# A recurrent block followed by cross attention: the attention's contexts dealt out over four steps instead of three

## The chip, the cores and the metric

The kernel runs on one core of one Trainium2 chip, in float32. The metric is the device time of one execution in microseconds; several executions are timed and the median is given. One further execution is taken by the hardware profiler.

The core's engines are called as in the profile: PE (TensorE, matrix multiplies and transposes), PEld (its weight loads), DVE (VectorE), ACT (ScalarE), POOL (GpSimd) and SP (SyncE, which issues all DMA transfers of this kernel, in order).

## The reference

The input `x` has 16 sequences of 128 tokens with 512 channels. Layer 0 is a recurrent block, layer 1 an attention between the channels of `x` and a second input `ctx` of the same shape (which also gives layer 0 its state). Cut to what matters:

```python
# layer 0
xa  = ln(x);  sx = shift(xa) - xa
xxx = einsum(tanh((xa + sx*maa_x) @ maa_w1), maa_w2)       # five mixtures
xk, xw, xv, xr, xg = xa + sx * (maa_stack + xxx)
w = exp(-exp(time_decay + tanh(xw @ td_w1) @ td_w2))
r, k, v, g = xr @ Wr.T, xk @ Wk.T, xv @ Wv.T, silu(xg @ Wg.T)
for t in range(128):                                       # 32 heads of 16
    out_t = r_t @ (u * k_t v_t + s);  s = k_t v_t + w_t * s
x1 = x + groupnorm(out) * g @ Wo.T
xc = ln(x1);  sx2 = shift(xc) - xc
x2 = x1 + sigmoid((xc + sx2*fr) @ Wfr.T) * (relu((xc + sx2*fk) @ Wfk.T)**2 @ Wfv.T)
# layer 1, per sequence; 128 "channels" x 512 "positions"
Mn = Wn @ inorm(x2) + bn
Mm = Wm @ inorm(ctx) + bm
A  = softmax(Mn.T @ Mm)
return Wo @ ((Wl @ ctx + bl) @ A.T) + bo + x2
```

What hangs on `ctx` alone in layer 1, `Mm` and the product of `Wo`, `Wl` and `ctx`, is called a context here. It does not depend on layer 0.

## The kernel before

The 16 sequences form 8 groups of two (`n = 2`, `G = 8`). A group passes through stages, each a generator that yields between portions:

- `stageB` (L227): first norm, shift and the matmuls `p1` (L245, L249) of the mixtures.
- `stageB2` (L268): the five mixtures `px` (L286), the projections `pj` (L224) with Wk, Wr, Wg and `pv` (L331) with Wv, and the decay (`pd`, `pw`).
- `stageR` (L358): the recurrence, in a form with pair products, masks and small matmuls (`pq` L405, `p4` L410, `pl` L456, `pu` L505, `pa` L526, `po` L533 and L538). It loads the state `s0` (L381), spreads keys into KX by eight DMAs (L425) and values into VX by four (L474).
- `stageC` (L568): transposes `py` (L580), the output projection and the channel mix: `ptk` (L594) with Wo, Wfr and Wfv, `pj` (L621) with Wfk.
- `stageX` (L759): loads a group's contexts back from DRAM.
- `stageL` and `stageLb` (L810, L772): the attention: `pn` (L779), and four times per sequence the scores `pS` (L785), their maximum on DVE (L787), the exponential on ACT (L789), the reciprocal (L790), scaling (L791), the transpose `pA` (L794) and its eviction (L797); after each second one `pO` (L803) and an addition (L805).
- `stageE` (L752) calls `context` (L732) for each sequence of the groups that it is given.

A context loads the sequence into `xs` (L737), takes statistics on DVE (L131, in `rownorm`, with a power on POOL) and normalizes on ACT (L145). `pm` (L741) and its eviction with bias (L742) give one half of `MVe`, four matmuls `pV` (L746) and a copy (L747) the other; L749 stores it to DRAM as `mvD`, of which there are 16. `xs` and `MVe` have no room of their own: by the number of the sequence in the group, they take the tiles of `yT` or `xk2`, and of `xcT` or `sx2`, which `stageC` uses otherwise. The two PSUM banks are those of the attention (`ls` and `la`):

```python
xs = sb1.tile([128, 512], FP, name="xs", tag=("yT", "xk2")[i])
mv = sb1.tile([128, 1024], FP, name="MVe", tag=("xcT", "sx2")[i])
```

The work goes in steps. Group g is in stage B at step g, in B2 at g + 1, R at g + 2, C at g + 3, X and L at g + 4; the last group's C and L are written apart (`stageCb`) and run at step 10, next to the second last group's attention. Within a step, `interleave` (L823) takes portions of the step's streams by a due time, which is the stream's delay (`DLY`) plus the share of its portions done. The contexts come with a delay of 1, after the others:

```python
if step in EARLY:
    gs = EARLY[step]
    streams.append((stageE(gs), 2 * len(gs), 1, (6, step)))
```

This is the order in which the instructions are traced. A scheduler then gives each engine its order: what was traced earlier comes first, but an instruction whose operands and buffers are free in the scheduler's own timing is drawn ahead. So work of a later portion can fill the gaps of an earlier one, across steps too. The engines then run these orders as they stand.

Of the kernel before, what the change touches and what calls it, by code (L numbers as in the profile page):

```python
# [26 lines left out]
OFF = [0, 1, 2, 3, 4, 4]  # L27
ORDER = [3, 4, 2, 1, 0, 5]
DLY = [-0.2, 0.2, 0.0, 0.4, 0.8, 0.4]
EARLY = {0: [0, 1], 1: [2, 3], 2: [4, 5, 6, 7]}  # L30
LASTX = 2


# [1 line left out]
def rwkv_xattn_kernel(ctx: ExitStack, tc: tile.TileContext, a: dict, out: bass.AP):  # L35
# [716 lines left out]
    def stageE(gs):  # L752

        for g in gs:
            for b in range(n):
                context(g, b)
                yield
# [87 lines left out]
    for step in range(G + max(OFF)):  # L845
# [5 lines left out]
        for k in ORDER:  # L851
            for g in range(G):
                if step_of(k, g) == step and not (g == G - 1 and k in (3, 4)):
                    streams.append((ST[k][0](g), ST[k][1], DLY[k], (k, g)))
# [3 lines that stand above are left out]
# [72 lines left out]
```

## Time and profile before

| | us |
|---|---|
| median of 3 runs | 971.24 |
| lowest and highest | 967.41, 981.34 |
| the profiled execution | 969.33 |
| its span (first to last instruction) | 967.5 |
| PE busy | 898.5 (93%) |
| DVE busy | 644.3 (67%) |
| ACT busy | 500.4 (52%) |
| first and last start of a context's `pm` | 21.2, 154.4 |
| first `pS` of the attention | 272.7 |

Busy times come from one profiled execution. The difference of span and time lies before the first and after the last instruction. A matmul in float32 is two entries on PE, and a run of them overlaps, so their lengths add up to more than the time that they take; the spacing of their starts is the time that counts.

In the views, `out<-in` names the tiles by the program's names without buffer numbers, and what stands behind an arrow in brackets is what ended an idle time.

### The profile page before, as it was taken

To read this page: it belongs to the slowest core of one execution; us is meant where nothing else is said; L and a number is where in the kernel's file an instruction comes from. 1 tells how busy PE (TensorE), PEld (TensorE's weight loads), DVE (VectorE), ACT (ScalarE), POOL (GpSimd) and SP (SyncE) were. 2 spreads that over 40 slices of the span, in tenths; PEclk is the share of its full clock that TensorE was granted. 3 is DMA by queue.
4 is the path that set the end of the run, shared out by engine and by line. 5 is a ranking of instruction groups with operands and counts; after the bars stand their busy time and mean duration, and the time that the engine had idled before them with its cause. 6 is when DMAs were issued, how large, how long until landed. Compare 5 with 4: busy or idle time off the path is not lost.

```text
span 967.5 us, 19263 instructions
## 1 busy us (share of the span) xinstructions
PE 898.5 (93%) x7556; PEld 613.0 (63%) x7556; DVE 644.3 (67%) x1599; ACT 500.4 (52%) x1057; POOL 59.2 (6%) x95
## 2 busy tenths in 40 slices
PE   4889999998989999999999999999989998997985
PEld 3666767667554867576756677585846565754643
DVE  5787677946586668875787578755784595942322
ACT  4675273443366445564565445734564265654544
POOL 5111010000000000010000000000000000000000
PEclk9999999999999999999999999999999999998998
DMA  6566647355413635253444524553445323344410
GB/s 200 182 239 215 200 154 247 96 158 190 142 55 72 206 123 179 60 173 110 140 115 132 190 86 131 147 182 102 131 112 145 139 66 113 96 155 142 152 44 23
DMA packets 77612, 134.04 MB, mean 139 GB/s; under 512 B 33825, under 2 KB 43681, under 8 KB 77520
## 3 DMA queue, kind: packets, MB, share of 16 engines
q1 hardware_dynamic: 77522, 132.81, 44.5%
q8 instruction: 60, 0.98, 0.4%
q14 instruction: 30, 0.25, 0.1%
HBM read 104.45 MB, written 22.04 MB: 131 GB/s over the span
## 4 chain that ended last, share of the span: by engine, by line
PE 64%; DVE 18%; ACT 7%; DMA 6%; SPq 3%; issue 2%; POOL 0%; DVEq 0%; ACTq 0%; POOLq 0%
PE ptk L594 14%; PE pj L224 11%; PE pv L331 5%; PE pj L621 5%; PE pO L803 4%; PE pl L456 4%; PE pS L785 4%; DVE PP L394 3%; PE pA L794 2%; PE ptl L674 2%; SPq L425 2%; DVE xm L289 2%; PE pu L505 1%; DVE xm L290 1%; PE po L533 1%
## 5 line engine op out<-in xcount | busy, mean ns | idle before, releaser
L224 PE MATMUL pj<-xm,wb 128*128 128x256 f32 x768 | 179.4, 386 | 2.9 <-DVE xm L289 2.8
L224 PEld LDWEIGHTS pj<-xm,wb 128*128 128x128 f32 x768 | 145.3, 193 | 28.3 <-issue 5.7
L143 POOL TENSOR_TENSOR rs<-rs,mhalf 128x1 f32<-128x1 f32 x64 | 40.8, 644 | 619.2 <-DVE rs L128 605.0
L785 PE MATMUL pS<-MV,Mn 128*128 128x512 f32 x112 | 62.9, 644 | 9.1 <-ACT e L789 5.2
L789 ACT ACTIVATE e<-pS,nm 128x512 f32<-128x512 f32 x64 | 44.3, 693 | 50.1 <-DVE nm L787 49.8
L787 DVE TENSOR_REDUCE nm<-pS 128x1 f32<-128x512 f32 x64 | 43.5, 685 | 40.1 <-PE pS L785 39.9
L803 PE MATMUL pO<-AT,MV 128*128 128x256 f32 x224 | 58.4, 399 | 1.9 <-ACT AT L797 1.9
L289 DVE TENSOR_TENSOR xm<-px,sx 128x512 f32<-128x512 f32 x80 | 53.6, 681 | 7.6 <-PE px L286 7.5
L331 PE MATMUL pv<-wb,xm 128*128 128x512 f32 x128 | 57.5, 597 | 0.2 <-DMA wb<-wvc 0.2
L797 ACT COPY AT<-pA 128x512 f32<-128x512 f32 x64 | 37.4, 585 | 39.1 <-PE pA L794 34.7
L791 ACT ACTIVATE e<-e,nm 128x512 f32<-128x512 f32 x64 | 46.4, 730 | 18.7 <-DVE nm L790 18.7
L290 DVE TENSOR_TENSOR xm<-xm,xaT 128x512 f32<-128x512 f32 x80 | 54.4, 684 | 0.5
L803 PEld LDWEIGHTS pO<-AT,MV 128*128 128x128 f32 x224 | 43.1, 198 | 17.8 <-issue 7.1
L621 PE MATMUL pj<-xk,wb 128*128 128x256 f32 x224 | 52.4, 383 | 0.0
L594 PE MATMUL ptk<-wb,kk 128*128 128x512 f32 x112 | 51.4, 596 | 0.9 <-DMA wb<-in_Wfv_dram 0.9
L456 PE MATMUL pl<-KX,r 128*32 128x128 f32 x1536 | 48.6, 274 | 3.3 <-DMA KX<-ks 3.0
L594 PE MATMUL ptk<-wb,sx 128*128 128x512 f32 x112 | 50.8, 598 | 0.0
L594 PE MATMUL ptk<-wb,yT 128*128 128x512 f32 x112 | 49.8, 596 | 0.8 <-DVE nm L790 0.8
L456 PEld LDWEIGHTS pl<-KX,r 128*32 128x32 f32 x1536 | 40.8, 110 | 14.1 <-issue 8.8
L794 PEld LDWEIGHTS pA<-ident,e 128*128 128x128 f32 x256 | 30.0, 141 | 30.6 <-issue 14.0
L805 DVE SCALAR_TENSOR_TENSOR x<-pO,cb,x 128x256 f32<-128x256 f32 x32 | 15.4, 480 | 49.5 <-PE pO L803 49.3
L286 PE MATMUL px<-sk,w2s 98*128 98x256 f32 x160 | 41.7, 356 | 5.4 <-ACT sk L264 2.0
(201 smaller groups left out, 1709.9 us busy)
## 6 DMA issues: line engine op xcount, KB each, us to landing
wb<-in_Wk_dram SPq DMA_DIRECT2D x16, 512.0 KB, 4.6
mvD<-MVe SPq DMA_DIRECT2D x16, 512.0 KB, 4.1
wb<-in_Wr_dram SPq DMA_DIRECT2D x16, 512.0 KB, 3.4
wb<-wvc SPq DMA_DIRECT2D x16, 512.0 KB, 3.6
wb<-in_Wg_dram SPq DMA_DIRECT2D x16, 512.0 KB, 4.2
wb<-in_Wo_dram SPq DMA_DIRECT2D x14, 512.0 KB, 3.4
wb<-in_Wfk_dram SPq DMA_DIRECT2D x14, 512.0 KB, 3.5
MV<-mvD SPq DMA_DIRECT2D x14, 512.0 KB, 3.8
```

The source lines that it names most:

```text
L224: nc.tensor.matmul(pj[:, m], lhsT=wb[:, m, cc, :], rhs=xm[:, cc], start=cc == 0, stop=cc == 3)
L289: nc.vector.tensor_tensor(xm[:, sl], px.rearrange("p c (b t) -> p c b t", b=n), sx[:, sl], ALU.mult)
L290: nc.vector.tensor_tensor(xm[:, sl], xm[:, sl], xaT[:, sl, :, 1:129], ALU.add)
L331: nc.tensor.matmul(pv, lhsT=xm[:, m, b], rhs=wbs[m // 2][:, m % 2], start=m == 0, stop=m == 3)
L456: nc.tensor.matmul(t[cs, 128 * cc : 128 * cc + 128], lhsT=r[:, cc, b, cs], rhs=KX[:, n * cc + b, :, 16 * c : 16 * c + 16], start=True, sto ...
L594: nc.tensor.matmul(pt, lhsT=act[:, m, b], rhs=wbs[m // 2][:, m % 2], start=m == 0, stop=m == 3)
L621: nc.tensor.matmul(pj[:, m], lhsT=wb[:, m, cc, :], rhs=xk2[:, cc], start=cc == 0, stop=cc == 3)
L785: nc.tensor.matmul(pS, lhsT=Mn[:, tsl], rhs=Mm, start=True, stop=True)
L789: nc.scalar.activation(e, pS, AF.Exp, bias=nm[:, 0:1], accum_out=nm[:, 1:2])
L791: nc.scalar.activation(e, e, AF.Identity, scale=nm[:, 2:3])
L794: nc.tensor.transpose(pA[:, sc], e[:, 128 * sc : 128 * sc + 128], ident)
L803: nc.tensor.matmul(pO, lhsT=Vc[:, sc], rhs=AT[:, sc], start=sc == 0, stop=sc == 3)
```

## The change

One table of the program is another one. Steps 0 to 2 had the contexts of two, two and four groups; now steps 0 to 3 have those of one, two, three and two groups. The code of a context, its tiles and its place in a step (after the others) are the same.

```diff
-EARLY = {0: [0, 1], 1: [2, 3], 2: [4, 5, 6, 7]}
+EARLY = {0: [0], 1: [1, 2], 2: [3, 4, 5], 3: [6, 7]}
```

Step 3 is the first in which `stageC` runs, for group 0.

## The prediction

> **What bounds the kernel now.** I read the profile's first page, then the busy times of each engine by stretches that follow the steps, then the instructions of the contexts, then TensorE's order of time where it stood still, and last the chain of waits. The page first: span, busy share of TensorE, and its busy tenths and granted clock over 40 slices of 24 us.
>
> ```profile
> span 967.5 us, 19263 instructions
> PE 898.5 (93%) x7556; PEld 613.0 (63%) x7556; DVE 644.3 (67%) x1599; ACT 500.4 (52%) x1057; POOL 59.2 (6%) x95
> PE   4889999998989999999999999999989998997985
> PEclk9999999999999999999999999999999999998998
> ```
>
> TensorE is busy 898.5 of 967.5 us; the other 69 us are at the start, in a few slices between, and at the end. The change moves matmuls and removes none, so the whole effect has to come out of these 69 us. The stretches say where they lie (length, busy time of TensorE, weight loads, VectorE, ScalarE, GpSimd, granted clock, DMA share):
>
> ```profile
> 0.00:100.00 100.00, 78.51 (x489) 56.03 (x490) 73.31 (x206) 57.81 (x115) 24.31 (x33) 0.97 0.65 212
> 100.00:160.00 60.00, 58.05 (x601) 44.23 (x600) 40.86 (x103) 29.73 (x63) 4.33 (x8) 0.99 0.60 189
> 160.00:230.00 70.00, 65.43 (x603) 48.06 (x603) 55.91 (x128) 26.41 (x65) 2.23 (x3) 0.96 0.56 162
> 260.00:300.00 40.00, 34.36 (x249) 20.22 (x247) 30.80 (x77) 25.32 (x58) 1.92 (x2) 0.96 0.21 54
> 300.00:500.00 200.00, 196.60 (x1794) 138.87 (x1794) 146.90 (x356) 105.47 (x227) 8.10 (x16) 1.00 0.45 138
> 800.00:968.00 168.00, 142.37 (x918) 87.68 (x916) 71.30 (x204) 87.59 (x180) 5.00 (x10) 0.95 0.32 104
> ```
>
> Length less busy gives TensorE's idle time: 21.5 us in the first 100, 2.0 in 100 to 160, 4.6 in 160 to 230, 5.6 in 260 to 300, 3.4 in 300 to 500 and 25.6 at the end; the stretches not shown hold the other 7. From 300 on TensorE sets the pace (98%), so work that comes late there costs its full length.
>
> Now the contexts: the two lines of their matmuls and statistics, with first and last start.
>
> ```profile
> L741 PE MATMUL pm<-l1n,wnm x32: 590/593/1223, 21.2 to 154.4; 128*128 128x512 f32 x32
> L131 DVE BATCH_NORM_STATS2 st<-xs x16: 656/690/695, 16.5 to 131.6; 128x6 f32<-128x512 f32 x16
> DMA to landing us min/median/max: 2.5/3.3/5.6
> ```
>
> All 16 contexts are through by 155 us (two `pm` passes each, so 32). They are filler: the first user, attention of group 0, starts near 271.
>
> TensorE around the gap before the second channel mix (start, length, instructions, and in brackets how long it stood idle before and for whom):
>
> ```profile
> 272.74 1.13 PE L785 MATMUL pS<-MV,Mn 128*128 128x512 f32 x2 [0.31 <-ACT Mn L781]
> 278.53 1.94 PE L785 MATMUL pS<-MV,Mn 128*128 128x512 f32 x2 [2.03 <-ACT e L789]
> 287.31 1.04 PE L580 MATMUL py<-ident,y 128*128 128x128 f32 x8
> 289.83 1.06 PE L405 MATMUL pq<-PP,emat 128*32 128x512 f32 x8 [1.49 <-DVE PP L394]
> 291.57 1.13 PE L785 MATMUL pS<-MV,Mn 128*128 128x512 f32 x2 [0.67 <-ACT e L789]
> 293.46 7.13 PE L594 MATMUL ptk<-wb,yT 128*128 128x512 f32 x16 [0.76 <-DVE nm L790]
> ```
>
> Four of these waits, 0.31 + 2.03 + 0.67 + 0.76 = 3.8 us of the 5.6, come from attention of group 0, pulled forward as filler here: each score block goes TensorE, VectorE, ScalarE and back, and the next waits for its bank.
>
> **The change part by part.** The scheduler decides places, so I read the built orders. *Contexts 0 to 11* (groups 0 to 5) stand on TensorE nearly where they stood: the third and fourth have within 1 us of the same matmul work ahead of them (number of matmuls by their spacing in this trace), the others 2 to 5 us less to 13 us more. The new numbers for steps 0 to 2 therefore hardly act; I price this at nothing, bounds -2 to +2, since the cover is only the loose start (21.5 us idle). *Contexts 12 to 15* (groups 6 and 7) do move: from 119 to 155 us to behind the first channel mix, between its last `ptk` with Wfv and `py` of group 1, which in this trace is 261 to 287.
>
> What they carry, from the chain of waits (start, length, step):
>
> ```profile
> 137.88 0.89 PE pV L746 x8
> 143.09 0.86 PE pm L741 x2
> 153.99 0.69 DVE Sx L490
> ```
>
> A context is 0.89 + 0.86 = 1.75 us of TensorE, four are 7.0. On VectorE 0.69 of statistics and some 0.4 of small operations, four 4.4; on ScalarE a normalization (0.81), and evictions of 0.69 and 0.58, four 8.3; on SyncE a load and a store each.
>
> *(1) Where they leave.* TensorE is busy 58.05 of 60 there. If everything behind moves up by 7.0, idle time does not change. But the chain of waits passes through VectorE for about 120 to 132 and 153 to 160 (its line above is one of many) and through SyncE's queue and the s0 load for 146 to 152: about 25 of the 60 us don't shorten by matmuls leaving. Holes of 0 to 7.0; by that share, less the 4.4 us which VectorE loses too, I take +2.
>
> *(2) What goes in the other direction.* The built order has, ahead of the first `p1` matmul of group 4 (302.6 us here), less attention of group 0: one `pn`, three `pS`, three sets of `pA` and one `pO` fewer. By the same spacing, 0.86 + 3 x 0.86 + 3 x 0.44 + 4 x 0.43 = 6.5 us. So at that point the new order is ahead by 6.5 us of work, which it does later, by some 490 us: the two orders have the same matmuls behind them from there to about 725. At 98% busy that costs 6.5 in full. Moving 7.0 out and 6.5 back is a wash: only the idle time counts.
>
> *(3) The gap at 260 to 300.* Contexts fill it in place of score blocks, and don't go back and forth between three engines for each 0.86 us of matmul. The two `pS` left there stand with the eight `ptk` of Wo (6.9 us) between them. Of the 3.8 us, 0 to 3.8 can go; the `pq` wait of 1.49 on VectorE stays. VectorE gets 4.4 and loses about 3.2 (three reductions of 0.68, reciprocals, one addition), ScalarE 8.3 against about 9.5. I take -3.
>
> *(4) New waits.* The contexts' `xs` lies in the tiles of `yT` and `xk2`, their `MVe` in those of `xcT` and `sx2`, all of which the channel mix uses from step 3 on. Context 12's load waits until Wfv's matmuls have read `kk` (261); context 14 reuses that slot, and then `yT` of group 1. SyncE issues in order: behind the first waiting load stand a Wr pair, the second Wo and the VX loads. Wr is needed about 11.5 us of matmuls after `kk` is free, and a load lands in 3.3: covered. A round is issue 0.33, landing 3.3, statistics and small ones 1.2, the rs power on GpSimd 0.64, normalization 0.81: 6.3 us, two rounds 12.6 against 26 until `py` (287.3). `gt2`, behind context 15 in `xk2`'s slot, has about 10 us of matmuls until the first `ptk` and needs some 5. Nothing, and without this cover: if each round takes 16 us with queues on busy engines, 2 x 16 - 26 = +6.
>
> *(5) The end.* From 725 the built orders part again; the last group's first `pq` has 17.6 us less work ahead, its `po` 3.0 more, its first score block 4.7 less. The last chain ends alike. Nothing, bounds -4 to +4 from these last two.
>
> In 260 to 300 the clock granted is 0.96 and in 300 to 500 it is 1.00: it sinks where TensorE has holes, 0.04 x 40 = 1.6 us in that stretch. I count one such loss fewer there and one more after 100 as nothing.
>
> The Trainium skill (TensorE: Matmul & The Clock Gate, section on the HAM clock gate) says that an idle window of about 3.4 us sets TensorE to half clock. It speaks against the change: filler taken from 100 to 160 would open such windows; but no single idle time in the rows above is that long, and the clock sank all the same, so the row is stricter than the rule. By the rule the holes of (1) cost nothing more, by the row 1.6 us.
>
> *Sum:* 0 + 2 + 0 - 3 + 0 + 0 = -1 us. The profiled execution took 969.33 (span 967.5 and 1.8 around it), so 968.3; the median of the three runs, 971.24, stands 1.9 above, so about 970.
>
> **Rivals.** *A, slower: the stretch after 100 isn't TensorE's.* VectorE and the s0 load hold the recurrence of group 0, all 7.0 us open as holes, nothing is gained at 280, and one or two half-clock losses of 1.6 follow: 971.2 + 7 + 2 = 980. For it: the VectorE runs in the chain. Against: TensorE had no hole from 104 to 131. It decides if `po` of group 0 starts no more than 2 us earlier than 143.9. *B, slower: the slots.* The two rounds last past 287 and `yT` of group 1 is late: 971.2 + 6 = 977. Against: twice the time they need. It decides when a round passes 13 us. *C, faster: the hole closes.* The 7.0 us move up in full, the 3.8 vanish and with them the 2.0 of 100 to 160: 971.2 - 5.8 = 965. For it: a context waits on no other context. Against: VectorE's 1.49. *D, it does not do what it says:* eleven or twelve of sixteen contexts stay where they were, and the last four are an even swap: 971.2, which differs from the forecast by less than the runs do.
>
> **How the numbers follow.** Forecast together with D, which can't be told from it, 0.55, own range 966 to 975; A 0.20; B 0.10; C 0.15. The bounds add up to 971.2 - 2 - 3.8 - 4 = 961 below and 971.2 + 2 + 7 + 6 + 4 = 990 above; not all of the upper ones fall together, so I take 961 to 983. The runs shown spread from 967.41 to 981.34, and about 2% (19 us) is what a measurement can tell from no change. Faster by that would need 951.8, which no case reaches (0.03); slower, 990.7, needs A and B together with the end (0.05); within, 0.92.
>
> **What would show it.** Right: `pm` of twelve contexts by about 100 us and of four between 255 and 290; `po` of group 0 5 to 10 us earlier; `p1` of group 4 about 5 us earlier; idle time of TensorE in 260 to 300 at 2 to 4 us instead of 5.6; from 500 to 725 the same time for the same work. Wrong: over 4 us of idle time in 100 to 160; a wait of `yT` or `ptk` on `gt2`, `xs` or `MVe`; an idle time at the end that differs from 25.6 by over 4.

## The result, and the profile after

| | before | after |
|---|---|---|
| median of 20 runs, us | 973.02 | 978.5 |
| lowest and highest | 967.41, 981.34 | 973.45, 983.76 |
| first profiled execution, time and span | 969.33, 967.5 | 983.76, 982.0 |
| second one, taken later | 969.14, 967.4 | 977.08, 975.3 |

The ratio is 1.0056, interval 1.0038 to 1.0074: 5.5 us slower. A profile is one execution: the two of before lie 4 us below the median, the first of after 5 above it, so the spans differ by 14.5 and 7.9 us where the medians differ by 5.5. In both pairs they part between 100 and 260 us above all.

The page of after, with the rows shown of before:

```profile
span 982.0 us, 19257 instructions
PE 899.9 (92%) x7556; PEld 618.0 (63%) x7556; DVE 645.4 (66%) x1599; ACT 501.6 (51%) x1057; POOL 61.6 (6%) x95
PE   4889987999899999999999999999989997997995
PEclk9989998999999999999999999999999999998999
```

The work is the same; the seventh slice (147 to 172 us) has fallen to 7 tenths, with the clock at 8. The stretches (columns as before):

```profile
100.00:160.00 60.00, 52.82 (x552) 40.78 (x553) 38.80 (x89) 23.18 (x52) 2.33 (x5) 0.91 0.46 140
160.00:230.00 70.00, 63.76 (x605) 46.59 (x604) 53.42 (x126) 27.21 (x65) 2.94 (x5) 0.95 0.47 136
230.00:260.00 30.00, 25.93 (x236) 17.24 (x236) 15.04 (x33) 9.82 (x16) 0.03 (x1) 0.94 0.60 196
260.00:300.00 40.00, 38.20 (x297) 26.71 (x294) 33.64 (x88) 25.86 (x55) 6.38 (x7) 1.00 0.49 163
300.00:500.00 200.00, 196.88 (x1757) 137.13 (x1756) 139.70 (x345) 107.09 (x229) 9.89 (x17) 1.00 0.44 131
814.00:982.00 168.00, 140.94 (x871) 87.44 (x869) 71.26 (x209) 86.99 (x179) 4.72 (x10) 0.96 0.32 104
```

The row of before for 230 to 260, which the prediction does not show:

```profile
230.00:260.00 30.00, 29.10 (x255) 19.28 (x254) 14.58 (x39) 10.77 (x18) 1.97 (x3) 1.00 0.46 152
```

TensorE's idle time in 100 to 160 is 7.2 us (2.0 before), in 160 to 230 it is 6.2 (4.6), and in 230 to 260 it is 4.1 (0.9). The clock has sunk in the first of these from 0.99 to 0.91 and in the last from 1.00 to 0.94. In 260 to 300 the idle time is 1.8 (5.6): that gap is filled. From 300 on little differs.

What TensorE waited for between 100 and 260 us (in total, times, longest):

```profile
PE px L286 <- DVE xm L289: 4.6, 2, 4.1
PE pj L224 <- DMA wb<-in_Wg_dram: 3.6, 1, 3.6
PE pj L224 <- DVE xm L290: 3.2, 1, 3.2
PE pV L746 <- ACT MVe L747: 2.1, 1, 2.1
PE pl L456 <- DMA KX<-ks: 2.0, 1, 2.0
```

In before the longest single wait of this view was 1.2 us. Two of the new ones, in TensorE's order of time:

```profile
149.97 6.43 PE L224 MATMUL pj<-xm,wb 128*128 128x256 f32 x16 [3.60 <-DMA wb<-in_Wg_dram]
...
157.43 3.62 PE L224 MATMUL pj<-xm,wb 128*128 128x256 f32 x16
...
170.26 9.12 PE L224 MATMUL pj<-xm,wb 128*128 128x256 f32 x28 [3.16 <-DVE xm L290]
```

Sixteen of these matmuls take 3.62 us at full clock. After the first stop they took 6.43; after the second, 28 took 9.12 instead of 6.3 (from 32 in 7.17 us, as before has them there). The stops cost 3.6 + 2.8 and 3.2 + 2.8 us. The granted clock (third column from the end) says why the matmuls were slow:

```profile
149.90:153.00 3.10, 3.03 (x7) 2.50 (x8) 1.96 (x4) 0.00 (x0) 0.00 (x0) 0.50 0.64 254
157.50:161.00 3.50, 3.50 (x19) 3.04 (x19) 2.13 (x6) 0.59 (x1) 0.00 (x0) 1.00 0.41 150
170.20:173.50 3.30, 3.24 (x8) 2.61 (x9) 3.30 (x6) 0.00 (x0) 0.00 (x0) 0.50 0.32 73
176.00:179.40 3.40, 3.40 (x18) 3.01 (x16) 1.65 (x7) 0.37 (x1) 0.00 (x0) 1.00 0.50 154
```

It is 0.50 behind each stop and 1.00 a few us later.

The longest wait of the view, 4.1 us for `xm`, is a third stop, at 251 us (3.8 in the second profile). VectorE stands there for the load of the state `s0` (L381), with the `xm` behind it in its order. In before VectorE waits 1.3 us for that load.

```profile
250.13 0.29 DVE L383 TENSOR_REDUCE sm<-s 128x8 f32<-128x128 f32 x1 [7.51 <-DMA s<-in_s_dram]
```

```profile
251.07 0.79 PE L286 MATMUL px<-sk,w2s 98*128 98x256 f32 x2 [4.07 <-DVE xm L289]
```

The second stop is explained by VectorE's order, and SyncE's beside it:

```profile
161.72 0.69 DVE L345 SCALAR_TENSOR_TENSOR gt<-gt,pj 128x512 f32<-128x512 f32 x1 [2.02 <-ACT gt L344]
...
164.62 1.29 DVE L289 TENSOR_TENSOR xm<-px,sx 128x512 f32<-128x512 f32 x2
167.93 1.67 DVE L150 SCALAR_TENSOR_TENSOR xq<-sx,vec,xaT 128x256 f32<-128x256 f32 x4 [2.02 <-DMA gD<-gt]
169.52 0.68 DVE L290 TENSOR_TENSOR xm<-xm,xaT 128x512 f32<-128x512 f32 x1
```

```profile
162.43 0.33 SPq L347 DMA_DIRECT2D gD<-gt  x1
```

`xq` of group 3 (L236) has the tile of `g` of group 1 (L343), both tagged `gt`. It may not be written before the store of `g` to DRAM (L347) has read it. The store is issued at 162.43, VectorE is at `xq` by 165.9 and stands until the store has landed at 167.9. Behind `xq` in VectorE's order is the mixture `xm` (L290) that TensorE's next projection reads. In before the same two instructions stood 5 us of VectorE work apart, with no wait at all:

```profile
156.52 0.68 DVE L345 SCALAR_TENSOR_TENSOR gt<-gt,pj 128x512 f32<-128x512 f32 x1
...
162.19 1.66 DVE L150 SCALAR_TENSOR_TENSOR xq<-sx,vec,xaT 128x256 f32<-128x256 f32 x4
```

My theory W after these rows: the loss is this wait at `xq`. It is made by the moved filler, through a later projection of `g`. Rivals: the two other buffers that came late (`MVe` room, the Wg load), the moved contexts as such, or the new end. The stop at 251 us belongs on this list too; no run takes it away alone.

### The profile page after: what moved, and what is told of

It reads as the page before. It is cut to its first block, busy times and chain, and to the rows that moved or that the text cites. A ratio compares the mean times of both kernels' runs of the same rounds, so it can differ in the third digit from the quotient of the medians.

```text
span 982.0 us, 19257 instructions
## 1 busy us (share of the span) xinstructions
PE 899.9 (92%) x7556; PEld 618.0 (63%) x7556; DVE 645.4 (66%) x1599; ACT 501.6 (51%) x1057; POOL 61.6 (6%) x95
## 4 chain that ended last, share of the span: by engine, by line
PE 63%; DVE 17%; DMA 9%; ACT 4%; SPq 4%; issue 2%; POOL 1%; DVEq 0%; ACTq 0%; POOLq 0%
PE ptk L594 12%; PE pj L224 11%; PE pv L331 6%; PE pj L621 5%; PE pO L803 5%; PE pS L785 4%; PE pl L456 4%; DVE PP L394 3%; SPq L425 2%; PE pA L794 2%; PE ptl L674 2%; DVE xm L289 2%; DVE xm L290 1%; PE pu L505 1%; PE pa L526 1%
## 5 line engine op out<-in xcount | busy, mean ns | idle before, releaser
L224 PE MATMUL pj<-xm,wb 128*128 128x256 f32 x768 | 182.2, 390 | 8.1 <-DMA wb<-in_Wg_dram 3.6
L143 POOL TENSOR_TENSOR rs<-rs,mhalf 128x1 f32<-128x1 f32 x64 | 44.5, 701 | 656.2 <-DVE rs L128 641.6
L785 PE MATMUL pS<-MV,Mn 128*128 128x512 f32 x112 | 59.0, 609 | 3.7 <-ACT e L789 2.5
L331 PE MATMUL pv<-wb,xm 128*128 128x512 f32 x128 | 59.5, 615 | 2.4 <-DVE rs L128 1.9
L803 PE MATMUL pO<-AT,MV 128*128 128x256 f32 x224 | 54.6, 384 | 0.9 <-ACT AT L797 0.9
L290 DVE TENSOR_TENSOR xm<-xm,xaT 128x512 f32<-128x512 f32 x80 | 54.1, 683 | 0.5
L794 PE MATMUL pA<-ident,e 128*128 128x128 f32 x256 | 40.6, 281 | 5.8 <-ACT e L791 5.1
```

Source lines behind the costliest of these rows:

```text
L143: D["pow"] = nc.gpsimd.tensor_tensor(rs, rs, mhalf[:, 0:1], ALU.pow).ins
L224: nc.tensor.matmul(pj[:, m], lhsT=wb[:, m, cc, :], rhs=xm[:, cc], start=cc == 0, stop=cc == 3)
L290: nc.vector.tensor_tensor(xm[:, sl], xm[:, sl], xaT[:, sl, :, 1:129], ALU.add)
L331: nc.tensor.matmul(pv, lhsT=xm[:, m, b], rhs=wbs[m // 2][:, m % 2], start=m == 0, stop=m == 3)
L785: nc.tensor.matmul(pS, lhsT=Mn[:, tsl], rhs=Mm, start=True, stop=True)
L794: nc.tensor.transpose(pA[:, sc], e[:, 128 * sc : 128 * sc + 128], ident)
```

## The experiments

Ratios are to the kernel before on the same chip, with 95% intervals.

### The change in two halves, and in smaller parts

The front alone: the first steps have one and two groups, the third five.

```diff
-EARLY = {0: [0, 1], 1: [2, 3], 2: [4, 5, 6, 7]}
+EARLY = {0: [0], 1: [1, 2], 2: [3, 4, 5, 6, 7]}
```

> Contexts of the first three steps dealt out as in the changed kernel (one group, two), but the last four contexts stay in step 2. Theory H (holes: the last four contexts, gone from 100 to 160 us, leave waits for weight loads and stores uncovered): no change, ratio 0.998 to 1.002, TensorE idle in 100 to 160 at 2 to 3 us. Rival F (the later start of the first twelve costs): the whole loss, ratio 1.004 to 1.007. Rival E (another order at the end costs): some of it, since this order shares part of the changed kernel's last steps.

1.0056 (1.0029 to 1.0082). The front deal alone costs as much as the whole change. Its VectorE shows the same wait, and TensorE the same stop:

```profile
DVE xq L150 <- DMA gD<-gt: 1.3, 1, 1.3
```

```profile
170.11 9.06 PE L224 MATMUL pj<-xm,wb 128*128 128x256 f32 x28 [2.42 <-DVE xm L290]
```

Its longest wait is another one, which the whole change does not have, at 254 us:

```profile
PE ptk L594 <- DMA wb<-in_Wfv_dram: 5.2, 1, 5.2
```

The last two groups alone:

```diff
-EARLY = {0: [0, 1], 1: [2, 3], 2: [4, 5, 6, 7]}
+EARLY = {0: [0, 1], 1: [2, 3], 2: [4, 5], 3: [6, 7]}
```

> Only the last four contexts go from step 2 to step 3; the first twelve are dealt out as before, and the order of the matmuls from the middle to the end is that of the kernel before. H: the whole loss, ratio 1.004 to 1.007, idle time of TensorE 5 us or more above that of before between 100 and 260, and 3 us below it in 260 to 300. F and E: no change, 0.998 to 1.002.

1.0053 (1.0024 to 1.0082). This also costs as much as the whole, without a wait at `xq`. TensorE's idle time in 100 to 260 is 5.0 us above that of before, and its longest wait is another:

```profile
PE ptk L594 <- DMA wb<-in_Wfr_dram: 2.9, 1, 2.9
```

So the halves do not add up: each built order meets waits of its own. Only group 7 moved:

```diff
-EARLY = {0: [0, 1], 1: [2, 3], 2: [4, 5, 6, 7]}
+EARLY = {0: [0, 1], 1: [2, 3], 2: [4, 5, 6], 3: [7]}
```

> Only the contexts of group 7 go to step 3, those of group 6 stay in step 2; the first steps are dealt out as before, and the order from the middle to the end is that of before. H (contexts that leave 100 to 160 uncover waits): half of the loss of the run that moved both groups, ratio 1.002 to 1.003. If the loss comes with the first context that leaves: 1.005. If the gap at 260 to 300 pays for two contexts: 0.996 to 1.000.

1.0134 (1.0098 to 1.017), worse than both groups moved. And only group 1 moved (`0: [0], 1: [1, 2, 3]`, the rest as before):

> One part of the first steps alone: the contexts of group 1 go from step 0 to step 1, all others stay where the kernel before has them. On TensorE the order is that of before but for a stretch of 67 matmuls near 60 us and for the last steps (from 725 us), whose order is the one of the run with only the first steps changed. Theory F1 (the loss of the first steps' deal comes before 300 us, where stores of MVe and the Wg load come late): no change, ratio 0.998 to 1.002, with the idle time of TensorE by 300 us within 2 us of before. Rival E (the other order at the end costs): the whole loss, 1.004 to 1.007, with the idle time growing after 725 us.

1.0022 (0.9992 to 1.0052), with no wait at `xq` in its trace: undecided.

### The amount of filler

Contexts of groups 6 and 7 left out; attention of these groups reads group 5's:

```diff
-EARLY = {0: [0, 1], 1: [2, 3], 2: [4, 5, 6, 7]}
+EARLY = {0: [0, 1], 1: [2, 3], 2: [4, 5]}
-nc.sync.dma_start(out=mv, in_=d["mvD"][b])
+nc.sync.dma_start(out=mv, in_=D[min(g, 5)]["mvD"][b])
```

> The kernel before without the last four contexts: groups 6 and 7 attend to the contexts of group 5, so 7.0 us of matmuls, the loads and the stores are left out and put nowhere else. If the stretch from 100 to 160 is TensorE's, as the prediction had it: 7 us faster, ratio 0.992 to 0.994. H: at most 2 us faster, 0.998 to 1.002, as the waits under the contexts come to light.

1.0009 (0.998 to 1.0038): four contexts, 7.0 us of matmuls, taken out of the early steps bring nothing back. The other way, four more contexts, which nothing reads, in step 3:

```diff
-mvD = dr.tile([128, 1024], FP, name="mvD", bufs=16)
+mvD = dr.tile([128, 1024], FP, name="mvD", bufs=20)
+        if step == 3:
+            streams.append((stageE([6, 7]), 4, 1, (6, step)))
```

> The kernel before with four contexts more: those of groups 6 and 7 are computed a second time in step 3, and the second copies are not read. Nothing is taken from 100 to 160. H: only the place in step 3 is paid, 7.0 us of matmuls less the 3 to 4 us of the gap that they fill: +3 to +4 us, ratio 1.003 to 1.004. Rival B (the shared tiles make the channel mix of group 1 wait): 7 + 6 us, ratio 1.010 or more, with a wait of yT or of the Wo matmuls on a context's tile.

1.0123 (1.0085 to 1.0162): 12 us for 7.0 us of matmuls. The ratio is in the range of rival B, but the wait that was to show B is not there: the longest on a context's tile is 0.9 us. Neither run fits a price for a context by itself. A taken or added one moves what stands around it.

### The other late buffers

`MVe` of groups 1, 3 and 5 in a tile ring of the weights, in the changed kernel:

```diff
-mv = sb1.tile([128, 1024], FP, name="MVe", tag=("xcT", "sx2")[i])
+mv = (sb if g % 2 and g < 6 else sb1).tile([128, 1024], FP, name="MVe",
+     **dict(tag="wc", bufs=2) if g % 2 and g < 6 else dict(tag=("xcT", "sx2")[i]))
```

> The changed kernel with room for four MVe tiles in place of two in the first three steps (the contexts of groups 1, 3 and 5 take the other weight ring, which the channel mix uses only later); the order of the matmuls is that of the changed kernel but for some 35 near 75 us. F1: TensorE's stop of 2.1 us near 100, for a copy to MVe that waits for the store of the tile's last contents, goes, and with it the lateness behind it: 2 to 5 us faster than the changed kernel, ratio to the kernel before 1.000 to 1.004. If MVe's room is not the cause: as the changed kernel, 1.004 to 1.007.

1.0032 (1.0008 to 1.0056). The ratio is in the range that I gave for `MVe` as the cause, but the interval reaches well into the other one: undecided. The wait for `MVe` fell from 2.1 us to 0.6, and another took its place, while the two of Wg and `xm` stayed (and the stop near 250 us, with 3.5):

```profile
PE pj L224 <- DVE xm L290: 2.7, 1, 2.7
PE pj L224 <- DMA wb<-in_Wg_dram: 2.5, 1, 2.5
PE pV L746 <- DMA xs<-in_ctx_dram: 2.3, 1, 2.3
```

Wg of groups 0 and 1 in that ring, so that it can be loaded earlier, in the changed kernel and in before:

```diff
-late = nm in ("Wo", "Wfk", "Wfr", "Wfv")
+late = free or nm in ("Wo", "Wfk", "Wfr", "Wfv")
-pj4 = proj("Wg", xm, m2)
+pj4 = proj("Wg", xm, m2, g < 2)
```

> The changed kernel with the Wg pairs of groups 0 and 1 in the other weight ring, which is empty until the channel mix of group 0: their loads need not wait for the matmuls with Wv. Theory W (between 140 and 180 us the Wg load is late, TensorE stops for 3.6 us and falls to half clock, the store of g is late and holds the next mixture's first operation on VectorE): the stop goes, idle time of TensorE in 100 to 160 falls from 7.2 to 3 us or less, and the time by 3 to 6 us: ratio to the kernel before 0.999 to 1.003. If the wait only passes to the next one on the list: 1.004 to 1.007.

> The same edit on the kernel before, where TensorE never waited for Wg in this stretch. W: no gain, 0.998 to 1.002. If any other built order is slower than that of before by some 5 us: 1.004 to 1.007.

1.011 (1.0084 to 1.0136) in the changed kernel, where I expected 0.999 to 1.003, and 1.0025 (1.0002 to 1.0048) in before. In the changed kernel the waits for Wg and at `xq` are both gone, and it is slower still: its built order is another one, with waits such as this:

```profile
PE pl L456 <- DVE rs L128: 3.9, 1, 3.9
```

So this run doesn't price the Wg load. In before with this edit VectorE stands 0.9 us at `xq`, and TensorE has no stop from it.

### The wait at `xq`, taken away

`xq` of group 3, and `thhl` after it, in the tile of `sx2` instead of that of `g`, in the changed kernel and, as a control, in before:

```diff
-xq = sb1.tile([128, 4, n, 128], FP, name="xq", tag="gt")
+xq = sb1.tile([128, 4, n, 128], FP, name="xq", tag="sx2" if g == 3 else "gt")
-hl = sb1.tile([128, 2, 2, NT], FPR, name="thhl", tag="gt")
+hl = sb1.tile([128, 2, 2, NT], FPR, name="thhl", tag="sx2" if g == 3 else "gt")
```

> The changed kernel with xq and thhl of group 3 in the tile of sx2, not in that of g: VectorE's xq no longer waits until the store of g has landed. On TensorE the order is that of the changed kernel up to some 150 us and again from 240 to 725. W: the stop of 3.2 us near 167 and the half clock behind it go, 3 to 6 us faster than the changed kernel: ratio to before 0.999 to 1.003. If not the cause: 1.004 to 1.007.

> The same edit on the kernel before, whose VectorE has work until the store has landed, and whose order stays but for 54 matmuls. No change, 0.998 to 1.002.

0.9997 (0.9975 to 1.0019), 972.27 us, against 0.9999 (0.9979 to 1.0019) for the control: the whole loss is gone, and where there is no wait the edit does nothing. TensorE in the edited changed kernel, up to the first `pq` (L405) of group 1:

```profile
146.14 3.72 PE L224 MATMUL pj<-xm,wb 128*128 128x256 f32 x16 [2.98 <-DMA wb<-in_Wg_dram]
...
159.43 7.17 PE L224 MATMUL pj<-xm,wb 128*128 128x256 f32 x32
...
166.76 1.06 PE L405 MATMUL pq<-PP,emat 128*32 128x512 f32 x8
```

The same `pq` in the first and in the second profile of the changed kernel:

```profile
179.54 1.06 PE L405 MATMUL pq<-PP,emat 128*32 128x512 f32 x8
```

```profile
174.19 1.06 PE L405 MATMUL pq<-PP,emat 128*32 128x512 f32 x8
```

The wait for Wg is still there with 2.98 us, so the stop itself is not what costs the 5.5, nor is the one for `MVe`, which has its 2.1 us here too. The 32 matmuls after `xq` run at full clock without a stop. Up to this `pq` the traces have TensorE's matmuls in the same order in both kernels, and VectorE's order differs in the place of `xq` alone. From the first matmul after the Wg wait to `pq` the changed kernel takes 29.6 us (27.8 in its second profile), the edited one 20.6. Of the 9.0 and 7.2 us between, the stop at `xq` and the slow matmuls behind it are 6.0 and 4.1. Nearly all the rest is the 16 matmuls after the Wg wait, which are at full clock here (3.72 us) and at half in both profiles of the changed kernel (6.43 and 6.59): up to 2.9 us of what came back may be that.

Behind `pq` the scheduler places some work anew, so the edit is not a pure removal there. The stop at 251 us goes as well: in the new order both `xm` stand ahead of the operation that waits for `s0`, and TensorE waits 0.7 us at most. What this is worth in the total can't be read off, but it is small or made up for elsewhere: the edited kernel is ahead of the two profiles by 12.8 and 7.4 us at that `pq`, and by 12.4 and 8.4 us at the first `p1` of group 5 (405.1 against 417.5 and 413.5).

The front deal alone with the same edit:

> The front deal alone (one group in the first step, two in the second, five in the third), with xq of group 3 in a tile of its own instead of the one that g of group 1 leaves. Theory W: the loss of 1.0056 that the front deal alone showed is the same wait at xq, so it goes: 0.997 to 1.001. Rival (the front deal's loss comes from the late loads of weights, the Wfv wait of 5.2 us among them): 1.004 to 1.007 as before the edit.

0.9958 (0.9934 to 0.9982), 969.32 us: the front's loss is gone too, the ratio is a little below W's range (0.997 to 1.001), and this is the one version faster than both kernels, by 0.4% of before. Its profile has a span of 968.4, so it does not show where that gain lies. In this run the Wfv wait of 5.2 us that the front deal had at 254 us is gone with the one at `xq`, so it does not tell these two apart.

### The wait at `xq`, put in

The converse, in the kernel before. First, two more whole stores of `g` of group 1:

```diff
-d["gD"] = gD
+d["gD"] = gD if g != 1 else [nc.sync.dma_start(out=dr.tile([128, 4, n, 128], FP,
+          name="gD2", bufs=2), in_=gt) for _ in range(2)] and gD
```

> The converse of the last run: the kernel before, with two further stores of group 1's g to scratch memory that nothing reads, issued on SP's queue ahead of the one that is used, and TensorE's order as it was. Leaving out: nothing, the added stores alone are new. Theory W (the loss of the changed kernel is VectorE standing at group 3's xq until the stores of g have landed, with the next mixture queued behind it and TensorE without work and then at half clock): three stores of 512 KB in place of one land later, so xq, which came without a wait in the kernel before, waits 2 to 6 us, TensorE stands near 165 to 170 and the matmuls after it run at half clock; 1.003 to 1.008. Rival (the wait is only where the loss shows, and the deal itself costs it): nothing of this deal is changed, so 0.998 to 1.002.

0.9995 (0.9968 to 1.0023), but `xq` did not wait. The last store landed at 165.9, 4.3 us after its issue, and VectorE came to `xq` at 167.1 only, since three instructions stand ahead of it here that stand behind it in before. A miss of mine, which tells nothing about W. So then one small store in pieces of 4 bytes:

```diff
-d["gD"] = gD
+d["gD"] = gD if g != 1 else (nc.sync.dma_start(out=dr.tile([16, 128], FP, name="gd2", bufs=1)
+          .rearrange("c p -> p c"), in_=gt[:, 3, 1, 0:16]), gD)[1]
```

> The kernel before with one further store of 16 elements a partition of group 1's g, turned round so that it goes out in pieces of 4 bytes, to scratch memory that nothing reads: little data, but slow to land, and TensorE's order as it was. The three whole stores of the run before this landed as early as one and made no wait; this is to make it. Theory W (VectorE standing at group 3's xq until g's stores have landed is what costs): if the fine store lands later than 5 us after its issue, xq waits by the difference, TensorE stands some 1 to 3 us near 165 and the matmuls behind it run at half clock: 1.001 to 1.006; without a wait at xq, 1.000. Rival (the wait only shows the loss, the moved contexts cost it elsewhere): 0.998 to 1.002 even where xq waits over 2 us.

1.0106 (1.0074 to 1.0137). VectorE, then TensorE:

```profile
171.10 1.67 DVE L150 SCALAR_TENSOR_TENSOR xq<-sx,vec,xaT 128x256 f32<-128x256 f32 x4 [9.31 <-DMA gd<-gt]
```

```profile
164.86 3.72 PE L224 MATMUL pj<-xm,wb 128*128 128x256 f32 x16
173.43 5.67 PE L224 MATMUL pj<-xm,wb 128*128 128x256 f32 x16 [4.85 <-DVE xm L289]
```

And with 32 elements in place of 16:

> The same with 32 elements a partition, twice the pieces and so about twice the time to land: the dose. Theory W: xq waits longer than in the run with 16 by several us and the time grows with it, 1.003 to 1.012, with the stop and the half clock of TensorE at the same place. Rival: 0.998 to 1.002 whatever the wait.

1.0183 (1.0151 to 1.0216):

```profile
179.77 1.67 DVE L150 SCALAR_TENSOR_TENSOR xq<-sx,vec,xaT 128x256 f32<-128x256 f32 x4 [17.54 <-DMA gd<-gt]
```

```profile
182.10 5.89 PE L224 MATMUL pj<-xm,wb 128*128 128x256 f32 x16 [13.17 <-DVE xm L289]
```

Both are above the ranges that I gave for W (1.001 to 1.006 and 1.003 to 1.012), as `xq` waited longer than I had reckoned with. TensorE's, VectorE's and ScalarE's orders are those of before (but for some `po` matmuls near 162 us that trade places between the two profiles of before as well). From the one to the other, 8.2 us more of wait cost 7.5 us more of time (0.0077 of 971.9; 8.1 by the medians). Nothing further down takes it up. TensorE had one projection of 3.72 us to do when VectorE stopped; the rest of the wait became a stop, and the half clock added 2.0 and 2.2 us (5.67 and 5.89 against 3.72). The rival, that the wait only shows a loss which the moved contexts make elsewhere, gave 0.998 to 1.002 and falls: a wait at this place does cost. That it makes up the whole loss of the changed kernel does not follow from these two runs, whose waits are four times as long and more. The small pieces also delayed other transfers (the Wo pair landed in 15.9 and 22.3 us instead of 7.6 in the run with whole stores), but no other single wait of TensorE over 1.2 us in 100 to 260 came of it.

### The same kernels once more

> The kernel before once more, for a second profile: how much of the difference of 14.5 us between the two profiled spans is that of the executions. The runs shown say 973; if the first profile was a quick execution, the idle time of TensorE by 300 us is 2 to 5 us above the first one's.

> The changed kernel once more, for a second profile of it: the wait at xq of group 3 and the matmuls at half clock behind it should stand within 0.5 us of the first profile's if they belong to the built order, and elsewhere, or not at all, if they were an accident of that execution.

The second profile of before has a span of 967.4, so without the idle time that I expected on top, and no wait at `xq`. That of the changed kernel has the wait again at the same instruction, smaller, with the stop and the slow matmuls. It stands 4.1 us earlier and not within the 0.5 us that I expected, as TensorE is 3.6 us earlier at the Wg wait already:

```profile
163.84 1.67 DVE L150 SCALAR_TENSOR_TENSOR xq<-sx,vec,xaT 128x256 f32<-128x256 f32 x4 [1.31 <-DMA gD<-gt]
```

```profile
146.42 6.59 PE L224 MATMUL pj<-xm,wb 128*128 128x256 f32 x16 [3.03 <-DMA wb<-in_Wg_dram]
...
166.16 7.86 PE L224 MATMUL pj<-xm,wb 128*128 128x256 f32 x28 [2.46 <-DVE xm L290]
```

Stop and slow matmuls at `xq` make 2.5 + 1.6 = 4.1 us here, 3.2 + 2.8 = 6.0 in the first profile; the medians differ by 5.5. The wait belongs to the built order, its size to the execution.

## Why the prediction was wrong, point by point

The time, 978.5, lies within the range (961 to 983), and the change is within 2%. But the forecast was 1 us less than before, and 5.5 us more came; that the range held is owed to its width.

*The step that failed: "Contexts 0 to 11", priced at nothing, bounds -2 to +2.* The front deal alone, which moves just these, cost 1.0056, some 5.5 us. I compared how much matmul work lies ahead of each context and found it nearly equal. That was the wrong measure: what changed is which loads and which VectorE instructions come late, and work ahead of a context doesn't show that. In its place the runs show VectorE standing at `xq` until the store of `g` has landed, with TensorE's next operand behind it: 6.0 and 4.1 us of stop and slow matmuls in the two profiles of the changed kernel.

*Term (1), "+2, holes of 0 to 7.0": the mechanism was near, the place and size not.* Idle time in 100 to 260 went from 7.4 to 17.5 us in the first profile and to 15.3 in the second, 10.1 and 7.9 more where the bound was 7.0, with half clock on top. The term fails without `xq` too: the last two groups alone cost 1.0053, and in that run's profile the idle time of this stretch is 5.0 us above that of before. I priced the cover that leaves by the share of the chain on VectorE, and did not ask which buffer is read late if `g` is late. The missing row was in the trace of before: `g` done at 157.2 (156.52 and 0.68), its store issued at 157.23, `xq` on the same tile at 162.19. A slack of 5 us against a store that took 5.5 and 4.8 us to land here, in the two profiles of the changed kernel, is no slack.

*Rival A's condition* (`po` of group 0 no more than 2 us earlier than 143.9) was not met: it started at 139.7, 4 us earlier, and in the second profile at 136.8. It was tested ahead of the place where the time was lost. A's time, 980, is near the result by luck: it had no gain at 280, and there was one. The sign "over 4 us of idle time in 100 to 160" was met with 7.2 (5.7 in the second profile).

*The clock.* I counted half-clock losses as nothing on balance. The trace shows them after each of the first two stops, 2.8 us each (3.0 and 1.6 in the second profile). By the rule that the prediction weighed there, stops shorter than about 3.4 us would have cost nothing more. The rows differ: matmuls at half clock came behind stops of 2.42, 2.46, 3.03 and 3.16 us, and the measurement decides. The page of the Trainium skill that I weighed there, TensorE: Matmul & The Clock Gate (section on the HAM clock gate), also says that its window runs freely and is not started by the program. That agrees with these rows: a stop of 2.98 us left the clock alone, one of 3.03 at the same place did not, and one of 2.42 was followed by half clock.

*Right: the gap of term (3); term (2) in part.* The contexts of groups 6 and 7 stand in the gap, in place of score blocks. TensorE there, in the changed kernel:

```profile
270.53 1.13 PE L741 MATMUL pm<-l1n,wnm 128*128 128x512 f32 x2
...
288.27 1.02 PE L741 MATMUL pm<-l1n,wnm 128*128 128x512 f32 x2
...
295.83 1.12 PE L785 MATMUL pS<-MV,Mn 128*128 128x512 f32 x2
```

The idle time of 260 to 300 fell by 3.8 (forecast 3). `p1` of group 4, forecast 5 us earlier, came 6.0 later (308.7 for 302.6; 305.0 in the second profile), but at 297.6, 5.0 earlier, where the wait at `xq` is taken away. That kernel also has the forecast's time: 0.9997 against a forecast of 0.999. This does not make the rest of the sum right. The order of that kernel is partly new, and the last two groups alone, the move that terms (1) to (3) price at -1, cost 1.0053. The sum looked for new waits on the contexts' own tiles alone, and each new order had others.

*Right: (4) and (5).* The views of the changed kernel name no wait on `gt2` or for a slot of contexts 12 to 15 that cost over 0.6 us from 260 us on. Idle time at the end is 27.1 against 25.6; from the last group's first `ptk` to the end of the span it is 149.9 us in before and 150.5 and 147.9 in the two profiles of the changed kernel, so the end is not the cause.

*What stays open:* how much of the 5.5 us is the half clock after the Wg load, which left with the `xq` edit though the wait did not (at most 2.9); what the stop for `s0` at 251 us costs, which left with it as well; what makes the last two groups alone and group 7 alone slower, where no wait at `xq` is in the trace; and where the 0.4% of the front deal with the edit comes from.

## What to carry to other kernels

Moved filler was priced here less by its own matmuls (7.0 us taken out brought nothing, 7.0 added cost 12) than by what it left uncovered: list, in the trace of before, every reuse of a tile whose release is a transfer's landing, and the slack of each; one with no more slack than a landing takes can open with any new order. A wait on an engine that isn't the bottleneck cost nearly its full length (8.2 us more wait, 7.5 us more time) where the bottleneck's next operand was queued behind it and no other work was at hand. If a wait is suspected, make it longer in the kernel before with the order kept as well as taking it away: edits that take waits away also rebuild the order.

## What was not expected of the hardware

- Half clock followed stops of 2.4 to 3.6 us: 28 matmuls in 9.06 us after 2.42, in 7.86 after 2.46, in 9.12 after 3.16, instead of 6.3. Whether it comes varies: 16 matmuls took 3.72 us after a stop of 2.98 and 6.59 after one of 3.03.
- A store of 8 KB in pieces of 4 bytes took about 14 us from issue to landing (157.1 to 171.1), one of 16 KB about 22 (157.6 to 179.8): some 8 us for every 2048 pieces, where 512 KB in large ones landed in 4.3.
- A built order is kept to closely: two profiles of before, on different occasions, agree within 0.3 us in the start of `po` of group 4 (562.1 and 561.9), while timed runs of the same kernel spread from 967.4 to 981.3.
